# A four-layer graph attention kernel on one core: the last layer's residual on GpSimd, two sets of layer-norm statistics later, attention vectors fetched a group sooner

## Chip, cores and metric

The kernel runs on one core of one Trainium2 chip. The metric is the device time of one execution in microseconds (us), given as the median of several runs. In the profile PE is TensorE (matmuls), PEld its weight loads, DVE is VectorE, ACT is ScalarE, POOL is GpSimd, and SP is the engine whose queue issues nearly all DMAs here. "L389" is line 389 of the kernel before.

## The reference

Sixteen graphs of 1024 nodes with 256 features share one adjacency matrix. Four layers of graph attention follow each other, each with a layer norm ahead of it and a residual after it:

```python
for each layer:
    h = maximum(layernorm(x), 0)
    q = h @ W                                  # layers 0, 2: 4 heads of 64; layers 1, 3: 1 head of 256
    e = leaky_relu(q @ a_src + (q @ a_dst)^T)  # one 1024 x 1024 matrix per head
    attn = softmax(where(adj, e, -inf))
    x = x + act(attn @ q)                      # act: elu in layers 0 to 2, relu in layer 3
```

All is float32. In layer 3 the activation is a plain relu, so its residual is x + max(y, 0).

## The kernel before

**Steps.** A step is one layer of one graph. The 64 steps run in an order written out in `order_of_steps` (L635): four graphs are in flight (streams 0 to 3), and layers of four heads and of one head alternate wherever possible. Counted from n = 0, the first steps are: 0, 1 and 2 are layer 0 of streams 0, 1, 2; 3 is layer 1 of stream 0; 4 is layer 0 of stream 3; 5 and 6 are layer 1 of streams 1 and 2; 7 is layer 2 of stream 0. Steps 0, 1, 2, 4 and 7 have four heads, steps 3, 5 and 6 have one. Steps of layer 3 are n = 10, 12, 14, 16 and so on, 16 in all.

**One step on the engines.** With 1024 nodes on 128 partitions there are C = 8 column blocks.

- *Preparation* (L229). `stats` (L236) runs eight BN_STATS on DVE over x. `combine` and `combine_end` (L259, L277) turn them into a scale and a shift with ten small instructions on POOL. `normalise` (L282) applies both on ACT, one half (four blocks) at a time. From step 2 on the transposing is done by DMA: `split` (L290) separates the 16-bit halves on ACT and issues a DMA transpose on SP, `merge` (L301) puts them together again on ACT. `project` (L321) multiplies with W on PE (L328) and ACT copies each bank out (L330); after each half POOL scales the result (L340). `factors` and `rows` (L344, L349) make the other attention factor, which goes to DRAM and comes back as a broadcast (`fetch`, L367); ACT copies it into PSUM (L384).
- *Weights* (L386). For each head and column block DVE makes one tile of 128 x 1024 attention weights (L389): 32 tiles for a step of four heads, 8 for one of one head. The pool holds 18 such tiles (`WBUFS`).
- *Aggregation* (L393). PE multiplies the tiles with the projected features (L405), in eight groups per step; ACT copies each group's bank out (L420). There are four such PSUM banks (`ps`), shared with the projections.
- *Finish* (L426). In the groups of the following step: DVE takes the reciprocal (L441), POOL divides (L452), and in layers 0 to 2 POOL clips (L454), ACT exponentiates (L458), DVE combines (L464) and POOL adds to x (L465). In layer 3 a single DVE instruction does relu and add (L467). Then `store` (L469) issues the two output DMAs on SP, and behind them the load of the next graph into the same x tile.

**Order.** Every engine works its instructions in program order, and the program writes that order out by hand (`manual_schedule`, L565). The main loop (L611) goes through the groups of all steps; group k of step n has the index 8n + k. In each it emits, in this order: the weight tiles still due, the group's matmuls, the due pieces of the previous step's finish (at L477: group of the following step for divide, two divisions, two exponentials, two adds), then anything in `later`, then the preparation pieces that are due (`prepare`, L496), then weight tiles ahead.

When a preparation piece is due is read from tables (L50 to L57) of 21 numbers, relative to 8(n - 2). Their places are: statistics of half 0, of half 1, the combine of both (used with four heads), normalise half 0, normalise half 1, split 0, merge 0, four projections, split 1, merge 1, four projections, factors, rows, fetch, end. Lines 541 to 557 choose a table for each step. Before the change steps 0 to 2 with four heads use `SOON` (steps 0 and 1 are in fact written out otherwise), later ones `FOUR`, or `SHORT` or `NEXT` when the stream's previous layer ends too late; steps of one head use `ONE` or `TIGHT`. So step 4 uses `FOUR` (base 16: statistics at 8, combine at 11, normalise at 16 and 17) and step 7 uses `SHORT` (base 40: statistics at 36, normalise at 40 and 41).

**Start.** Masks are made from the adjacency matrix in eight blocks (`mask_rows`, L187): fetch, sign on DVE (L197), `turn` by PE into PSUM (L211), `positive` on DVE (L214), `nonzero` on ACT (L218). `order` (L582) interleaves them with the preparation of step 0.

**Vectors of later layers.** `weight_columns` (L134) makes the extra columns of W from the attention vector of a layer in four pieces: `vectors`, a DMA on SP (L143) into a tile of the weight pool; `spread`, a matmul on PE (L150) that copies it to all partitions, and an ACT copy (L153); `columns` on DVE (L160, L161); and `bound` (L169). For layers 1, 2 and 3 they are placed by the loop at L608, at indices 1, 27 and 43 and at 1, 2 and 8 groups after.

Of the kernel before, what the change touches and what calls it, by code (L numbers as in the profile page):

```python
# [32 lines left out]
ALU = mybir.AluOpType  # L33
# [16 lines left out]
FOUR = (-8, -8, -5, 0, 1, 0, 3, 5, 5, 5, 5, 1, 4, 5, 5, 5, 5, 6, 8, 8, 10)  # L50
SHORT = (-4, -4, -4, 0, 1, 0, 3, 5, 5, 5, 5, 1, 4, 5, 5, 5, 5, 6, 8, 8, 10)
NEXT = (-4, -4, -4, 1, 3, 2, 5, 8, 8, 8, 8, 4, 7, 8, 8, 8, 8, 9, 10, 10, 12)
ONE = (2, 2, 2, 3, 4, 3, 5, 7, 7, 7, 7, 4, 7, 8, 8, 8, 8, 8, 11, 11, 12)
SOON = (0, 0, 0, 1, 2, 1, 3, 4, 4, 5, 5, 2, 5, 6, 6, 7, 7, 7, 8, 8, 10)
FIRST = (-4, -4, -4, -2, -0.9, -1, -1, -0.8, -0.8, -0.8, -0.8, 0, 0, 1, 1, 1, 1, 1, 2, 2, 4)
TIGHT = (4, 4, 4, 5, 6, 5, 7, 8, 8, 8, 8, 6, 8, 9, 9, 9, 9, 9, 10, 10, 12)
LATE = (0, 0, 0, 1, 2, 1, 3, 4, 4, 4, 4, 2, 4, 5, 5, 5, 5, 5, 6, 6, 8)  # L57
# [11 lines left out]
def kernel(ctx: ExitStack, tc: tile.TileContext, x, adj, ws, avs, out):  # L69
    nc = tc.nc  # L70
# [38 lines left out]
    L = len(LAYERS)  # L109
# [312 lines left out]
    def slack(n):  # L422

        return LAYERS[steps[n + 1][1]][0] == 1

    def finish(n):  # L426

        b, l = steps[n]
        H = LAYERS[l][0]
        D = F // H  # L430
        st = state[n]

        def views(half):
            s = slice(half * HALF, (half + 1) * HALF)
            return (xs[b][:, s, :].rearrange("p c (h d) -> p (c h) d", h=H),
                    st["y"][:, s, :, 0:D].rearrange("p c h d -> p (c h) d"),
                    st["r"][:, s, :].rearrange("p c h -> p (c h)"))

        def divide():
            st["r"] = small.tile([P, C, H], F32, name="r")  # L440
            nc.vector.reciprocal(st["r"], st["y"][:, :, :, D])  # L441

        def scaled(half):
            xh, yh, r = views(half)
            rb = r[:, :, None].to_broadcast([P, HALF * H, D])
            if l < L - 1:

                e = st["e", half] = prep.tile([P, HALF * H, D], F32, name="rows",
                                                    bufs=HBUFS)
                if H > 1 and slack(n):  # L450
                    nc.vector.scalar_tensor_tensor(e, yh, 0.0, rb, op0=ALU.min, op1=ALU.mult)  # L451
            nc.gpsimd.tensor_tensor(yh, yh, rb, op=ALU.mult)  # L452
            if l < L - 1 and not (H > 1 and slack(n)):
                nc.gpsimd.tensor_scalar(e, yh, 0.0, -3.0e38, op0=ALU.min, op1=ALU.max)  # L454

        def exponential(half):
            if l < L - 1:
                nc.scalar.activation(st["e", half], st["e", half], AF.Exp)  # L458

        def add(half):  # L460
            xh, yh, r = views(half)
            if l < L - 1:
                e = st["e", half]
                nc.vector.scalar_tensor_tensor(e, e, -1.0, yh, op0=ALU.add, op1=ALU.max)  # L464
                nc.gpsimd.tensor_add(xh, xh, e)  # L465
                return
            nc.vector.scalar_tensor_tensor(xh, yh, 0.0, xh, op0=ALU.max, op1=ALU.add)  # L467

        def store(half):  # L469
            nc.sync.dma_start(  # L470
                out=out[b].rearrange("(p c) f -> p c f", p=P)[:, half * HALF:(half + 1) * HALF],
                in_=xs[b][:, half * HALF:(half + 1) * HALF, :])
            if half == 1 and b + STREAMS < B:
                load(b + STREAMS)


        at = (0, 0, 0, 0, 1, 1, 1) if slack(n) and H > 1 else (0, 0, 1, 1, 2, 2, 3)  # L477
        return list(zip(at, (divide, lambda: scaled(0), lambda: scaled(1), lambda: exponential(0),
                             lambda: exponential(1), lambda: add(0), lambda: add(1)))) + (
                    [(4, lambda: store(0)), (4, lambda: store(1))] if l == L - 1 else [])  # L480

# [37 lines left out]
    def emit_heads(i):  # L519

        while done["g"] <= min(i + C // 2, done["tiles"] + C, len(tiles) - 1):
            n, h, _ = tiles[done["g"]]
            if n >= done["prepared"]:
                break
            broadcast(n, h)
            done["g"] += C
            fetch_heads()
# [13 lines left out]
    for n, (b, l) in enumerate(steps):  # L541

        free = -99
        if b % STREAMS in last:
            over = last[b % STREAMS] + 1
            free = 8 * over + (8 if l == 0 else 2 if LAYERS[steps[over][1]][0] == 1 else 4)
        last[b % STREAMS] = n
        start = 8 * (n - 2)
        kind = ONE if LAYERS[l][0] == 1 else SOON if n < 3 else FOUR
        if kind is FOUR and free > start + kind[0]:  # L550
            kind = SHORT if slack(n - 2) else NEXT
        if kind is ONE and free > start + kind[0]:
            kind = TIGHT
        if free > start + kind[0]:
            kind = LATE
            start = max(free, agenda_of[-1][0] + 5, start - LATE[7])
        agenda_of.append([start + k for k in kind] if n > 1 else FIRST)
        if n > 2:


            assert agenda_of[n][7] >= 8 * (n - 2)
            assert agenda_of[n][3] >= agenda_of[n - 1][12]
    ending = []
    later = {}
    with tc.manual_schedule():  # L565
        blocks = [mask_rows(c) for c in range(C)]
        layer = [weight_columns(l) for l in range(L)]
        layer[0][0](nc.scalar)
        load(0, 2)
        load_weights(0)  # L570
        for c in range(C):
            blocks[c][0]()
        load(1)
        load_weights(1)
        for i in range(2, STREAMS):
            load(i)
        nc.scalar.activation(warm, half1, AF.Exp)
        nc.vector.tensor_copy(identb, ident)
        layer[0][1]()
        first = [piece for _, piece in preparation(0)]  # L580

        order = (  # L582

            [first[0], first[1], first[3], lambda: layer[0][2](range(1)), first[2],
             lambda: layer[0][2](range(1, K)), first[5], first[6], first[4], layer[0][3]]

            + [blocks[c][1] for c in range(4)]
            + [first[7], first[8], blocks[0][2], blocks[4][1], blocks[5][1], blocks[0][3],
               first[9], first[10], blocks[1][2], blocks[6][1], blocks[7][1], blocks[1][3],
               first[11], first[12], blocks[2][2], blocks[0][4],  # L590
               lambda: prepare(-4), first[13], first[14], blocks[1][4], blocks[2][3],
               blocks[3][2], first[15], first[16], blocks[3][3]]

            + [first[17], blocks[4][2], first[18], first[19], lambda: emit_heads(0),
               blocks[5][2], blocks[6][2], blocks[4][3], blocks[4][4], blocks[5][3], blocks[5][4],
               blocks[6][3], blocks[7][2], blocks[2][4], blocks[3][4], blocks[7][3],
               lambda: prepare(-2), blocks[6][4], lambda: prepare(-1), blocks[7][4]])
        plan(1)
        planned = 2
        done["prepared"] = 1  # L600
        for piece in order:
            piece()
        emit_tiles(C, must=True)
        prepare(-0.5)
        for i in range(2, STREAMS):
            load_weights(i)

        for l, at in ((1, 1), (2, 8 * 3 + 3), (3, 8 * 5 + 3)):  # L608
            for i, piece in zip((0, 1, 2, 8), layer[l]):
                later[at + i] = piece  # L610
        for n in range(len(steps)):  # L611
            for k, (h, i0, per) in enumerate(groups(n)):
                while planned < len(steps) and min(
                        a[0] for a in agenda_of[planned:planned + 2]) <= 8 * n + k:
                    plan(planned)
                    planned += 1
                emit_tiles(place[n, h, C - 1] + 1, must=True)
                aggregate(n, h, i0, per)
                if i0 + per == C:
                    done["free"] = place[n, h, C - 1] + 1  # L620
                while ending and ending[0][0] <= k:
                    ending.pop(0)[1]()
                upto = min(done["tiles"] + (6 if per > 1 else 3), done["free"] + WBUFS)

                emit_heads(upto - 1 + (C // 2 if per == 1 and k >= C - 2 else 0))
                if 8 * n + k in later:
                    later[8 * n + k]()
                prepare(8 * n + k)
                emit_tiles(upto)
            for _, piece in ending:  # L630
                piece()
            ending = finish(n) if n < len(steps) - 1 else []
# [35 lines left out]
```

## Time and profile before

| what | us |
|---|---|
| median of 3 runs | 2464.47 (2461.95 to 2467.52) |
| the profiled execution's own time | 2463.54 |
| its span, first to last instruction | 2461.8 |
| PE busy on matmuls | 2396.4 (97% of the span) |
| DVE busy | 2041.2 (83%) |
| ACT busy | 1484.9 (60%) |
| POOL busy | 1074.7 (44%) |
| L389, a weight tile on DVE | 1280 of 1.273 each |
| L467, the last layer's residual on DVE | 30 of 1.215 each |
| L452, L454, L465 on POOL | 2.091, 1.041 and 2.365 each |

A group of the profile is one line, engine and shape, with its count, busy time and the mean of one. A "wait" is idle time of an engine just before an instruction, put down to what released it. The chain is followed back from the last instruction to what released each one. A timeline line gives start and duration in us, the engine, the line, what is written and read, the number of instructions, and in brackets the idle time before. Matmul ends are modelled, and a matmul's busy time can contain a slower clock; the granted clock of a stretch is listed with 1.00 for full speed.

### The profile page before, as it was taken

Reading aid. Unit: us, or ns where it says so; the run is one execution under the profiler, and the core shown is the slowest. Engines: PE = TensorE matmul, PEld = TensorE weight load, DVE = VectorE, ACT = ScalarE, POOL = GpSimd, SP = SyncE. Lnnn points to the kernel's source line nnn. Section 1 sums busy time; section 2 is a strip of 40 time slices with the busy share of each in tenths; the row PEclk is TensorE's granted clock in tenths of the full one; section 3 lists DMA queues with packets and bytes.
Section 4 is the critical chain, followed back from the end, with each engine's and each line's share of the span. In section 5 each row is a group of like instructions: output and inputs, shape, how many; then the busy total and the mean of one; then the engine's idle time right before and its main releaser. Section 6 shows DMA issues by size and latency. Waiting matters only on the chain.

```text
span 2461.8 us, 86525 instructions
## 1 busy us (share of the span) xinstructions
PE 2396.4 (97%) x39104; PEld 2150.2 (87%) x39104; DVE 2041.2 (83%) x2138; ACT 1484.9 (60%) x2501; POOL 1074.7 (44%) x1366
## 2 busy tenths in 40 slices
PE   7989999999999999999999999999999999999899
PEld 5888798889898889898898888899988889888878
DVE  8988688888888988888988888988888888888963
ACT  5464676555666656765556765656665556765461
POOL 3344455543345454444343555453444344553341
PEclk9999999999999999999999999999999999999999
DMA  4322232233333322232433332323433422323221
GB/s 181 81 54 62 44 79 62 70 105 90 94 85 87 74 64 56 67 79 88 113 97 81 77 71 62 79 63 80 113 79 87 109 58 54 79 62 70 77 48 61
DMA packets 294761, 193.40 MB, mean 79 GB/s; under 512 B 264182, under 2 KB 266998, under 8 KB 292472
## 3 DMA queue, kind: packets, MB, share of 16 engines
q1 hardware_dynamic: 294382, 187.86, 30.2%
q8 instruction: 306, 5.01, 0.8%
q14 instruction: 63, 0.52, 0.1%
q10 hardware_dynamic: 10, 0.00, 0.0%
HBM read 105.39 MB, written 17.43 MB: 50 GB/s over the span
## 4 chain that ended last, share of the span: by engine, by line
PE 82%; ACT 6%; DVE 5%; DMA 4%; issue 2%; POOL 0%; SPq 0%; DVEq 0%; ACTq 0%
PE bank L405 64%; PE bank L328 18%; DVE w L389 4%; ACT rows L286 2%; DMA gs<-grow 2%; DMA grow<-gT 1%; ACT rows L295 1%; ACT g L384 1%; ACT rows L458 1%; ACT rows L303 1%; DVE bn L241 1%; ACT y L420 0%; DMA rows<-rows 0%; PE bank L352 0%; DVE rows L464 0%
## 5 line engine op out<-in xcount | busy, mean ns | idle before, releaser
L405 PE MATMUL bank<-whx,w 128*64 128x65 f32 x36864 | 1899.5, 240 | 26.4 <-DVE w L389 17.0
L405 PEld LDWEIGHTS bank<-whx,w 128*64 128x64 f32 x36864 | 1746.2, 144 | 186.5 <-issue 22.6
L389 DVE SCALAR_TENSOR_TENSOR w<-g,rcol,mask 128x1024 f32<-128x1024 f32 x1280 | 1538.9, 1273 | 206.1 <-PE bank L405 160.8
L340 POOL TENSOR_TENSOR whx<-whx 128x1024 f32<-128x1024 f32 x128 | 244.9, 1913 | 823.8 <-ACT whx L338 823.8
L420 ACT ACTIVATE y<-bank 128x260 f32<-128x260 f32 (+1 forms) x504 | 191.9, 381 | 567.1 <-PE bank L405 567.0
L328 PE MATMUL bank<-wx,rows 128*128 128x264 f32 (+1 forms) x2048 | 489.3, 393 | 16.0 <-ACT y L420 8.4
L328 PEld LDWEIGHTS bank<-wx,rows 128*128 128x128 f32 x2048 | 384.4, 192 | 92.5 <-ACT y L420 14.2
L452 POOL TENSOR_TENSOR y<-y,r 128x1024 f32<-128x1024 f32 x126 | 262.4, 2091 | 254.0 <-DVE rows L451 186.6
L330 ACT ACTIVATE whx<-bank 128x264 f32<-128x264 f32 (+1 forms) x512 | 193.6, 388 | 194.2 <-PE bank L328 193.5
L286 ACT ACTIVATE rows<-x,shift,rstd 128x256 f32<-128x256 f32 x512 | 264.5, 588 | 72.5 <-POOL shift L280 70.3
L465 POOL TENSOR_TENSOR x<-x,rows 128x1024 f32<-128x1024 f32 x96 | 227.1, 2365 | 181.6 <-DVE rows L464 181.6
L303 ACT ACTIVATE rows<-rows 128x2048 uint16<-128x2048 uint16 x124 | 265.9, 2144 | 21.5 <-DMA rows<-rows 21.5
L295 ACT ACTIVATE rows<-rows 128x2048 uint16<-128x2048 uint16 x124 | 236.9, 1911 | 3.9
L464 DVE SCALAR_TENSOR_TENSOR rows<-rows,y 128x1024 f32<-128x1024 f32 x96 | 187.9, 1957 | 49.1 <-ACT rows L458 43.7
L241 DVE BATCH_NORM_STATS2 bn<-x 128x6 f32<-128x256 f32 x512 | 175.5, 409 | 33.4 <-POOL x L465 30.0
L384 ACT ACTIVATE g<-gs 128x1024 f32<-128x1024 f32 x159 | 162.6, 1023 | 63.8 <-DMA gs<-grow 49.1
L274 POOL TENSOR_TENSOR rstd<-rstd,neghalf 128x4 f32<-128x4 f32 (+1 forms) x97 | 120.3, 1240 | 15.2 <-DVE shift L275 7.8
L458 ACT ACTIVATE rows<-rows 128x1024 f32<-128x1024 f32 x96 | 100.6, 1048 | 2.0 <-POOL rows L454 2.0
L441 DVE RECIPROCAL r<-y 128x32 f32<-128x32 f32 (+1 forms) x63 | 17.2, 274 | 96.3 <-ACT y L420 96.3
L451 DVE SCALAR_TENSOR_TENSOR rows<-y,r 128x1024 f32<-128x1024 f32 x58 | 70.1, 1250 | 1.1
L467 DVE SCALAR_TENSOR_TENSOR x<-y,x 128x1024 f32<-128x1024 f32 x30 | 36.5, 1215 | 8.9 <-POOL y L452 8.9
L338 ACT ACTIVATE whx<-whx,nbias 128x16 f32<-128x16 f32 (+1 forms) x128 | 40.3, 315 | 4.2
(67 smaller groups left out, 444.4 us busy)
## 6 DMA issues: line engine op xcount, KB each, us to landing
gs<-grow SPq DMA_DIRECT2D x159, 512.0 KB
x<-in_x SPq DMA_DIRECT2D x15, 1024.0 KB
out<-x SPq DMA_DIRECT2D x30, 512.0 KB
w<-in_adj SPq DMA_DIRECT2D x8, 512.0 KB
rows<-rows SPq DMA_TRANSPOSE x124
x<-in_x SPq DMA_DIRECT2D x2, 512.0 KB
wx<-in_L_gnn_W SPq DMA_DIRECT2D x8, 128.0 KB
out<-x SPq DMA_DIRECT2D x8, 128.0 KB
```

The lines of the kernel that those rows point to most:

```text
L241: nc.vector.bn_stats(bn[:, c, :], xs[b][:, c, :])
L286: nc.scalar.activation(xn[:, :, q, :], xs[b][:, c, :].rearrange("p (k i) -> p k i", k=K), AF.Relu, bias=st["shift"][:, c:c + 1], scale=st[ ...
L295: nc.scalar.activation(bits, xn.rearrange("p (n s) -> p s n", s=2), AF.Copy)
L303: nc.scalar.activation(st["hT", half].rearrange("p k i -> p (k i)").bitcast(U16).rearrange("p (n s) -> p n s", s=2), st["turned", half].re ...
L328: nc.tensor.matmul(pw, lhsT=st["hT", half][:, k, q * P:(q + 1) * P], rhs=wx[l][:, k, :], start=(k == 0), stop=(k == K - 1))
L330: nc.scalar.activation(st["whx"][:, c, :], pw, AF.Copy)
L340: nc.gpsimd.tensor_tensor(wh[:, :, :, 0:D], wh[:, :, :, 0:D], wh[:, :, :, D:D + 1].to_broadcast([P, HALF, H, D]), op=ALU.mult)
L389: nc.vector.scalar_tensor_tensor(w, state[n]["g", h], state[n]["rcol"][:, jc, h:h + 1], masks[LAYERS[steps[n][1]][3]][:, jc, :], op0=ALU.m ...
L405: nc.tensor.matmul(acc[o % P:o % P + cols, q, :], lhsT=st["w", h, jc][:, o:o + cols], rhs=st["whx"][:, jc, h * (D + 1):(h + 1) * (D + 1)], ...
L420: nc.scalar.activation(st["y"][:, i0:i0 + per, h, :], acc, AF.Copy)
L452: nc.gpsimd.tensor_tensor(yh, yh, rb, op=ALU.mult)
L465: nc.gpsimd.tensor_add(xh, xh, e)
```

## The change

Four edits are made.

1. In layer 3, `scaled` gets one more POOL instruction per half, max(y, 0), and `add` is a POOL add of x and y in place of DVE's combined instruction. The last step, which writes its result in another way (L409), is not concerned.
2. The table `SOON` is changed, and is used for all steps of four heads below n = 8, not below n = 3. So steps 2, 4 and 7 are placed by it. (A guard falls back to `SHORT` where the stream is not free; none of the three needs it.) Step 2 has its merges at 4 and all projections at 5, its factors at 6. Step 4 has its statistics and combine at 16 (was 8 and 11), normalise at 17 and 18 (was 16 and 17), splits at 17 and 18 (16 and 17), merges at 20 and 20 (19 and 20), projections at 21 as before. Step 7 has statistics and combine at 40 (was 36), normalise and splits at 41 and 42 (40 and 41), merges at 44 and 44 (43 and 44), projections at 45 as before.
3. At the start, mask block 5 is turned ahead of step 0's factors and rows, and no longer behind them.
4. The `vectors` piece of layers 2 and 3 is placed at 26 and 42, not 27 and 43; `spread`, `columns` and `bound` keep their places.

```diff
-SOON = (0, 0, 0, 1, 2, 1, 3, 4, 4, 5, 5, 2, 5, 6, 6, 7, 7, 7, 8, 8, 10)
+SOON = (0, 0, 0, 1, 2, 1, 4, 5, 5, 5, 5, 2, 4, 5, 5, 5, 5, 6, 8, 8, 10)
...
             nc.gpsimd.tensor_tensor(yh, yh, rb, op=ALU.mult)
+            if l == L - 1:
+                nc.gpsimd.tensor_scalar(yh, yh, 0.0, 3.0e38, op0=ALU.max, op1=ALU.min)
...
-            nc.vector.scalar_tensor_tensor(xh, yh, 0.0, xh, op0=ALU.max, op1=ALU.add)
+            nc.gpsimd.tensor_add(xh, xh, yh)
...
-        kind = ONE if LAYERS[l][0] == 1 else SOON if n < 3 else FOUR
+        kind = ONE if LAYERS[l][0] == 1 else SOON if n < 8 else FOUR
         if kind is FOUR and free > start + kind[0]:
             kind = SHORT if slack(n - 2) else NEXT
+        if kind is SOON and free > start:
+            kind = SHORT
...
-            + [first[17], blocks[4][2], first[18], first[19], lambda: emit_heads(0),
-               blocks[5][2], blocks[6][2], blocks[4][3], blocks[4][4], blocks[5][3], blocks[5][4],
+            + [first[17], blocks[4][2], blocks[5][2], first[18], first[19], lambda: emit_heads(0),
+               blocks[6][2], blocks[4][3], blocks[4][4], blocks[5][3], blocks[5][4],
...
-        for l, at in ((1, 1), (2, 8 * 3 + 3), (3, 8 * 5 + 3)):
-            for i, piece in zip((0, 1, 2, 8), layer[l]):
+        for l, at in ((1, 1), (2, 8 * 3 + 2), (3, 8 * 5 + 2)):
+            for i, piece in zip((0, 1, 2, 8) if l == 1 else (0, 2, 3, 9), layer[l]):
```

## The prediction, made before the changed kernel ran

> Steps are counted from 0, groups as 8n + k; the "fifth and eighth step" are n = 4 and n = 7. All times are microseconds of the profiled execution before, or are shifted from them.
>
> **What bounds the kernel now.** First the page: busy shares, then the chain that ended last.
>
> ```profile
> PE 2396.4 (97%) x39104; PEld 2150.2 (87%) x39104; DVE 2041.2 (83%) x2138; ACT 1484.9 (60%) x2501; POOL 1074.7 (44%) x1366
> ...
> PE 82%; ACT 6%; DVE 5%; DMA 4%; issue 2%; POOL 0%; SPq 0%; DVEq 0%; ACTq 0%
> ```
>
> PE is the bound; a saving on DVE or ACT counts only where PE waits for it. Second, what PE waited for:
>
> ```profile
> PE bank L405 <- DVE w L389: 17.0, 22, 0.9
> ...
> PE bank L150 <- DMA w<-in_L_gnn_a: 7.0, 3, 4.6
> ```
>
> Third, busy time by stretch. From 299 to 2280 us PE idles 16 of 1981 us, and the waits there name DVE for 0.6 us. So almost nothing can be won in the middle; the edits can count before 299 us and after 2280 us. Fourth, the timelines of those two ends, and the chain around 200 us:
>
> ```profile
> 200.91 2.82 DMA w<-in_L_gnn_a
> 203.73 0.14 issue
> 203.87 1.24 PE bank L150 x2
> ```
>
> PE stands for 1.30 us (202.56 to 203.87) for the attention vector of layer 2. The clock after it:
>
> ```profile
> 202.00:204.00 2.00, 0.70 (x4) 1.00 0.58 210
> 204.00:206.00 2.00, 2.00 (x4) 0.67 0.01 4
> 206.00:208.00 2.00, 2.00 (x6) 0.50 0.16 34
> ```
>
> The column after the busy time is the granted clock: it halves, and the 48 matmuls that follow take 12.11 us where 48 take 10.43 elsewhere, 1.68 us more. DVE at the end:
>
> ```profile
> 2288.04 1.22 DVE L467 SCALAR_TENSOR_TENSOR x<-y,x 128x1024 f32<-128x1024 f32 x1
> 2289.17 2.70 DVE L241 BATCH_NORM_STATS2 bn<-x 128x6 f32<-128x256 f32 x8
> 2291.79 2.46 DVE L389 SCALAR_TENSOR_TENSOR w<-g,rcol,mask 128x1024 f32<-128x1024 f32 x2
> 2294.16 1.21 DVE L467 SCALAR_TENSOR_TENSOR x<-y,x 128x1024 f32<-128x1024 f32 x1
> 2295.30 7.24 DVE L389 SCALAR_TENSOR_TENSOR w<-g,rcol,mask 128x1024 f32<-128x1024 f32 x6
> ```
>
> No gap on DVE, and PE waits tile by tile until 2302.59: both residual adds lie on the path here.
>
> **What the Trainium skill says.** "TensorE: Matmul & The Clock Gate", Part 1: the array runs at half rate after an idle window of about 3.4 us, in windows that run freely. The trace agrees on the half rate and about 3.3 us of it, but 1.30 us of standing was enough at 203.9, while 1.17 us at 287 was not; so a stall may cost 1.7 us more or nothing. "GPSIMD Engine Reference", 4.1: two-input elementwise about twice as slow as VectorE, one-input near line rate. Agrees: L465 2365 ns against L467 1215; L454 1041. Same page, section 1: GpSimd shares its SBUF interface with VectorE instructions of two SBUF inputs. Agrees: L464 takes 1.21 us alone, 2.9 beside L452.
>
> **Part 1, the last layer's residual (15 steps, 30 halves).** DVE loses 30 x 1.215 = 36.5 us. POOL gains per half one TENSOR_SCALAR at 1.04 (L454's row) and one add at 2.37 (L465's row, same shapes): 102 us in all, 6.8 a step. What is queued behind: in a middle step (496 to 519 us) POOL sits idle 20.4 us from the second L452 to the next L340. Added there are one or two scalars and two adds, under 7 us; cover 13 us, and if it were gone each microsecond would cost up to 15 in the kernel. The adds need no lookahead tiles of DVE ahead of them and end near 504, before DVE's 508.4. The two stores (509.08) wait on SP behind the fetch issued at 508.69, so they and the load behind them (516.79) stay. PE gain in the middle: 0. At 2288 the cover is POOL's 7.9 us before the statistics; 1.04 + 2.37 fit. There DVE gets 1.13 + 1.22 = 2.3 us back, PE waits 2.3 less, and the later waits to 2361 hang on the same tiles. **+2.3** (bounds 1 to 2.6: the next g copy on ACT, at 2302.71, moves only about 1.5). In the last step DVE's adds end at 2446.1 and their stores leave by 2449.4; POOL, with two L452, two scalars and two adds (10.6 us) from 2434.8, ends at 2445.4: 0.
>
> **Part 2, block 5 turned earlier.** DVE waits 1.68 us for that block at 33.34, then does three masks. With the block turned behind block 4 (30.4 to 31.0), one mask of 1.15 us runs inside the wait; the next waits for block 6 (33.2) as before. DVE starts its tiles 1.15 us sooner and has no gap from 36.94 to 159 us, so this carries on. Step 2's new places (all projections at 5, merges at 4) fall where PE waits for DVE: 0, unless the merge at 4 keeps ACT from the g copy that DVE needs at 81 (I find 0.5 us to spare; loss up to 1).
>
> **Part 3, step 4's statistics from group 8 to 16.** The 8 BN_STATS (2.65 us at 100.36) leave the stretch in which PE waits for DVE (109 to 137 us). With part 2, step 2's first group ends at 137.4, not 141.2. ACT's normalise and split of step 4 (148.0 to 151.9) no longer stand before the evictions of step 3's projections, so group 2 of step 2 starts at 148.7, not 154.44: 5.7 us won so far. Then it is given back. POOL does, in program order, L452, L454, L340 (to 147.5) and only then step 4's combine (4.2 us, as at 49.41 to 53.60): 151.7. ACT: normalise and split to 155.75, evict and exponential, second normalise and split to 161.25. On SP the two transposes now stand around step 3's store and fetch of its g row (issued near 160, 165.74 before), which step 3 needs only at 170: no cost. A transpose lands 5.2 to 6.2 us after its split (876.7 to 882.2, 2066.65 to 2072.85): 166.75. Merge 2.15, g copy 1.0, then the eviction of group 5: 170.2. PE ends group 5 at 164.6, has banks for three projections (0.92 each, to 167.4), stands 2.8 us, needs five more: 174.8, or 176.5 with a half clock. Before: 177.26. **+1.5** (0 to 5.3, the upper end without the stall).
>
> **Part 4, vectors a group sooner, layer 2.** At group 26 they stand behind the g fetch that goes out near 198, not the one at 200.46; 2.82 us of transfer end near 201.3, before PE is done at 202.56. Both the 1.30 and the 1.68 go. Late next: merge of step 5 at 213.3, projections would start at 214.3. **+3.0** (0 to 3.0). Layer 3: at group 42 the fetch is behind the first transpose of step 7, which now leaves at 283 (part 5) and takes 1.9 to issue; it lands at 286.7, against 286.96. +0.4 at most.
>
> **Part 5, step 7's statistics from 36 to 40.** In the trace they run on DVE at 253.03, after the last tile of step 4: no wait of PE ends there, so nothing is won. Moved, the combine stands on POOL behind two L452 and step 6's second L340, which waits for ACT until 273.0: 279.1 instead of 260. ACT's normalise starts there, not at 273.44; second split to 287.4, landing 292.9, merge 295.05, g copy, eviction of group 5 at 296.35. PE has issued three projections by 294.0, stands 2.35 and ends at 300.95, or 302.6 at half clock, against 298.98. **-3.0** (+0.4 to -4).
>
> **Sum.** 2.3 + 1.5 + 3.0 - 3.0 = 3.8 us. The profiled execution took 2463.54 (span 2461.8, 1.7 around it): 2459.7. It lies 0.9 below the median of the runs (2464.47), so I forecast **2460.6**, 0.16% less. A measurement tells about 0.2% (4.9 us, 2459.5) from no change.
>
> **Rivals.** (B) The stalls of parts 3 and 5 do not form: transposes or combine come earlier than worked out. For it: steady steps split and merge two groups apart with PE waiting 0 to 1 us; against: POOL's order is fixed by the program. 5.3 + 3.0 + 0.4 + 2.3 = 11.0: 2453.5; with one stall of two some 2457.5. (C) Slower: the second halves of steps 4 and 7 land later still. Place: SP's in-order queue, where one transpose took 5.31 us to issue at 71.02 instead of 1.9 and the g fetches stand between. Each microsecond of delay costs two, one per step; with 3.8 to use up, slower by 4.9 needs 4.4 us at each, a landing 9.9 us after the split. 2470. Against it: no landing over 6.2 us is seen where a merge waited. (D) The vector fetch does what it says but lands no sooner (it still queues behind a fetch): 2.3 + 1.5 - 3.0 = 0.8: 2463.7.
>
> **Chances.** Forecast (2458 to 2464) 0.50, of it 0.15 under 2459.5; B 0.30, nearly all faster; C 0.10, 0.08 of it slower; D 0.10, same. Faster 0.43, same 0.49, slower 0.08. Range 2453 to 2465: it takes in B's end and D, leaves C.
>
> **What would show it.** Right: no PE wait at L150 near 200 us and full clock there; L389 without L467 between at about 2288 and PE there 2.3 us earlier; PE waits on L328 of 2 to 3 us in steps 2 and 5, released by ACT, with half clocks after. No wait at L328 in those two steps, with ACT's normalise starting the moment it is issued and not when POOL releases it, speaks for B. Wrong altogether: PE waits in steps 11 to 17 that name POOL, or stores that leave later than the g fetch before them.

## The result and the profile after

The changed kernel takes **2471.36 us** in the median of 16 runs, the kernel before 2465.21 beside it (16 runs): ratio **1.0021**, 95% interval 1.0013 to 1.0030. It is slower by about 5 us. The forecast was 2460.6 us, 0.16% less than before. The profiled execution after took 2468.03 us (span 2466.1), 4.5 us more than the one before.

The page, in the two lines that were read before: DVE has lost its 30 residual instructions and POOL has gained 170 us, but PE is as busy as it was, and still holds the chain of work that ended last (81%, 82% before).

```profile
PE 2398.5 (97%) x39104; PEld 2152.4 (87%) x39104; DVE 2010.0 (82%) x2108; ACT 1485.7 (60%) x2501; POOL 1245.1 (50%) x1426
...
PE 81%; DVE 6%; ACT 5%; DMA 5%; issue 2%; POOL 1%; SPq 0%; DVEq 0%; ACTq 0%; POOLq 0%
```

What PE waited for in the changed kernel (total, times, longest):

```profile
PE bank L328 <- ACT y L420: 17.0, 12, 4.4
PE bank L405 <- DVE w L389: 12.9, 18, 0.9
...
PE bank L150 <- DMA w<-in_L_gnn_a: 4.9, 1, 4.9
...
PE bank L150 <- ACT y L420: 1.8, 1, 1.8
```

The waits for DVE (17.0 before) and for the vectors (7.0, 3 times, before) are smaller, as intended. The first line is new in size: before it had 8.4 us, the longest 2.5. L328 is the projection; it waits because its PSUM bank is not yet copied out, and the copy, L420, is on ACT.

**Where the time went.** PE transposes one row tile per step (L352); the start of that instruction in both traces dates each step. After minus before, in us (minus is sooner):

| from the transpose of step ... to that of ... | change in this stretch | forecast |
|---|---|---|
| start to 1 (mask block) | -2.3 | -1.15 |
| 1 to 2 (second projections of step 2) | +2.8 | 0 |
| 2 to 4 (statistics and merges of step 4) | +0.9 | -1.5 from the start to step 4, mask included |
| 4 to 5 (vectors of layer 2) | -3.0 | -3.0 |
| 5 to 6 | +1.4 | 0 |
| 6 to 7 (step 7) | +4.3 | +3.0, less 0.4 |
| 7 to 60 (middle) | +2.2 | 0 |
| 60 to 63 (end) | -2.0 | -2.3 |

The sum is +4.3; the spans differ by 4.4. The end and the vectors came out as forecast. The losses stand in steps 2, 4 and 7, whose places are changed. Two rows hold chance of one execution, too. In the first, three of the five traces without the mask edit (res_only, vec_only, step7_vec) are ahead of the kernel before, too, by 1.1 to 1.5 us. And the +1.4 from step 5 to 6 goes with a half clock from 250.5 us that lasts 6.83 us, where the kernel before has one of 3.41.

**The stall in step 2's group 5** (changed kernel; timeline, the lines of ACT and PE that concern it: start, duration, engine, line; in brackets the idle time before and what ended it):

```profile
169.10 2.14 ACT L303 ACTIVATE rows<-rows 128x2048 uint16<-128x2048 uint16 x1 [3.89 <-DMA rows<-rows]
171.15 1.00 ACT L384 ACTIVATE g<-gs 128x1024 f32<-128x1024 f32 x1
172.10 0.36 ACT L420 ACTIVATE y<-bank 128x260 f32<-128x260 f32 x1
...
172.51 6.15 PE L328 MATMUL bank<-wx,rows 128*128 128x264 f32 x20 [3.85 <-ACT y L420]
```

L303 is the second merge of step 4. ACT reaches it at 165.2 and stands 3.89 us for its DMA transpose. The g copy (L384) and the eviction (L420) are behind it in ACT's program, although what the eviction copies was ready long before: PE ended its three projections at 168.66 and stands 3.85 us for that bank. Then the 20 matmuls of the five projections left take 6.15 us, where 20 take 4.72 at full clock later in the trace. The kernel before does all eight projections (32 matmuls) at this place without a stop:

```profile
169.88 7.39 PE L328 MATMUL bank<-wx,rows 128*128 128x264 f32 x32
```

The same picture stands earlier in the changed kernel, in step 0's groups, with step 2's second merge, which begins at 76.92:

```profile
76.92 2.15 ACT L303 ACTIVATE rows<-rows 128x2048 uint16<-128x2048 uint16 x1 [5.07 <-DMA rows<-rows]
78.98 1.00 ACT L384 ACTIVATE g<-gs 128x1024 f32<-128x1024 f32 x1
79.92 0.36 ACT L420 ACTIVATE y<-bank 128x260 f32<-128x260 f32 x1
80.01 7.25 DVE L389 SCALAR_TENSOR_TENSOR w<-g,rcol,mask 128x1024 f32<-128x1024 f32 x6 [1.05 <-ACT g L384]
...
80.34 6.15 PE L328 MATMUL bank<-wx,rows 128*128 128x264 f32 x20 [4.37 <-ACT y L420]
```

Here DVE, too, waits for the g copy, 1.05 us. The split ahead of that transpose ended at 68.0, and the merge could start at 76.9, 9 us later: on SP its issue stood behind two g fetches until 68.93 and took 4.54 us.

**Step 7** loses in another way, ahead of its projections:

```profile
279.00 2.07 ACT L286 ACTIVATE rows<-x,shift,rstd 128x256 f32<-128x256 f32 x4 [2.41 <-POOL shift L280]
...
287.15 0.37 ACT L420 ACTIVATE y<-bank 128x257 f32<-128x257 f32 x1
287.54 1.52 PE L150 MATMUL bank<-w,ones 1*128 1x512 f32 x2 [1.78 <-ACT y L420]
...
288.98 6.64 PE L405 MATMUL bank<-whx,w 128*128 128x257 f32 x16
```

POOL releases the normalise at 279.00, as worked out (279.1). ACT then normalises and splits twice without a pause to 287.15, an eviction is due inside that, and PE's matmul at L150, which needs the bank, stands 1.78 us. The kernel before stood there for the vectors' DMA:

```profile
287.10 1.09 PE L150 MATMUL bank<-w,ones 1*128 1x512 f32 x2 [1.17 <-DMA w<-in_L_gnn_a]
288.12 3.74 PE L405 MATMUL bank<-whx,w 128*128 128x257 f32 x16
```

What follows costs more than the stall. The clock, of the changed kernel (stretch, length, PE busy and matmuls, granted clock, DMA share, GB/s):

```profile
204.00:206.00 2.00, 2.00 (x7) 1.00 0.30 102
...
288.00:290.00 2.00, 2.00 (x4) 0.52 0.81 156
...
294.00:296.00 2.00, 2.00 (x9) 0.78 0.24 90
```

Around 204 us the clock is full now, and the stall for the vectors of layer 2 is gone: that is the 3.0 us of part 4. From 288 it is halved, and the 16 matmuls take 6.64 us instead of 3.74.

Both costs can be summed over two-microsecond stretches from 40 to 312 us: PE's idle time, and PE's busy time times one minus the granted clock. Before: 17.3 idle and 8.1 lost to the clock. After: 19.9 and 12.0. So of the 6.5 us that this stretch got worse, 3.9 are clock.

**DVE at the end** of the changed kernel, where two L467 stood among the tiles:

```profile
2289.59 4.85 DVE L389 SCALAR_TENSOR_TENSOR w<-g,rcol,mask 128x1024 f32<-128x1024 f32 x4
2294.36 2.70 DVE L241 BATCH_NORM_STATS2 bn<-x 128x6 f32<-128x256 f32 x8
2296.97 9.62 DVE L389 SCALAR_TENSOR_TENSOR w<-g,rcol,mask 128x1024 f32<-128x1024 f32 x8
```

The tiles follow each other, and the next transposes are 2.0 us nearer than before.

### The profile page after: what moved, and what is told of

It is laid out like the page before. It is cut to its first block, busy times and chain, and to the rows that moved or that the text cites. A ratio compares the mean times of both kernels' runs of the same rounds, so it can differ in the third digit from the quotient of the medians.

```text
span 2466.1 us, 86566 instructions
## 1 busy us (share of the span) xinstructions
PE 2398.5 (97%) x39104; PEld 2152.4 (87%) x39104; DVE 2010.0 (82%) x2108; ACT 1485.7 (60%) x2501; POOL 1245.1 (50%) x1426
## 4 chain that ended last, share of the span: by engine, by line
PE 81%; DVE 6%; ACT 5%; DMA 5%; issue 2%; POOL 1%; SPq 0%; DVEq 0%; ACTq 0%; POOLq 0%
PE bank L405 63%; PE bank L328 17%; DVE w L389 4%; DMA gs<-grow 2%; DMA grow<-gT 2%; ACT rows L286 2%; ACT rows L295 1%; DMA rows<-rows 1%; ACT g L384 1%; ACT rows L460 1%; DVE bn L241 1%; ACT rows L303 0%; ACT y L420 0%; PE bank L352 0%; DVE w L160 0%
## 5 line engine op out<-in xcount | busy, mean ns | idle before, releaser
L405 PE MATMUL bank<-whx,w 128*64 128x65 f32 x36864 | 1901.5, 241 | 24.9 <-DVE w L389 12.9
L405 PEld LDWEIGHTS bank<-whx,w 128*64 128x64 f32 x36864 | 1747.8, 144 | 184.5 <-issue 26.5
L420 ACT ACTIVATE y<-bank 128x260 f32<-128x260 f32 (+1 forms) x504 | 191.6, 380 | 564.7 <-PE bank L405 564.7
L328 PE MATMUL bank<-wx,rows 128*128 128x264 f32 (+1 forms) x2048 | 489.1, 393 | 22.7 <-ACT y L420 17.0
L328 PEld LDWEIGHTS bank<-wx,rows 128*128 128x128 f32 x2048 | 385.2, 192 | 99.2 <-ACT y L420 22.9
L467 POOL TENSOR_TENSOR x<-x,rows 128x1024 f32<-128x1024 f32 x96 | 227.1, 2366 | 174.6 <-DVE rows L466 174.6
L303 ACT ACTIVATE rows<-rows 128x2048 uint16<-128x2048 uint16 x124 | 265.9, 2145 | 30.1 <-DMA rows<-rows 28.2
L384 ACT ACTIVATE g<-gs 128x1024 f32<-128x1024 f32 x159 | 162.6, 1023 | 65.1 <-DMA gs<-grow 56.1
L454 POOL TENSOR_SCALAR y<-y 128x1024 f32<-128x1024 f32 x30 | 109.0, 3633 | 2.6
L469 POOL TENSOR_TENSOR x<-x,y 128x1024 f32<-128x1024 f32 x30 | 65.4, 2202 | 0.0
```

What stands on the lines that cost most here:

```text
L303: nc.scalar.activation(st["hT", half].rearrange("p k i -> p (k i)").bitcast(U16).rearrange("p (n s) -> p n s", s=2), st["turned", half].re ...
L328: nc.tensor.matmul(pw, lhsT=st["hT", half][:, k, q * P:(q + 1) * P], rhs=wx[l][:, k, :], start=(k == 0), stop=(k == K - 1))
L405: nc.tensor.matmul(acc[o % P:o % P + cols, q, :], lhsT=st["w", h, jc][:, o:o + cols], rhs=st["whx"][:, jc, h * (D + 1):(h + 1) * (D + 1)], ...
L420: nc.scalar.activation(st["y"][:, i0:i0 + per, h, :], acc, AF.Copy)
```

## The experiments

Theory after the result: the new places put a second merge on ACT ahead of an eviction; ACT holds its whole queue for the transpose, PE stands for the bank, and the clock halves after. Rivals: the residual on POOL slows the middle (+2.2 us stand there); a stall in one step only replaces one in a later step; the losses are chance of the clock. Every kernel computes the whole reference. Each ratio is against the kernel before on the same chip, whose medians were 2462.0, 2459.4, 2460.6 and 2460.9 us in the four sets. In kernels with a table of their own (STEP) all lines after it are one higher: L328 is L329, L420 is L421.

**1. Residual, mask and vectors, all places old** (old_tables).

```diff
-SOON = (0, 0, 0, 1, 2, 1, 4, 5, 5, 5, 5, 2, 4, 5, 5, 5, 5, 6, 8, 8, 10)
+SOON = (0, 0, 0, 1, 2, 1, 3, 4, 4, 5, 5, 2, 5, 6, 6, 7, 7, 7, 8, 8, 10)
...
-        kind = ONE if LAYERS[l][0] == 1 else SOON if n < 8 else FOUR
+        kind = ONE if LAYERS[l][0] == 1 else SOON if n < 3 else FOUR
```

> Everything of the change except the tables: steps 2, 4 and 7 are placed as before. Theory (the new places make ACT hold a merge for a transpose while PE's bank waits for an eviction behind it, in steps 0, 2 and 5): with those stalls gone the residual's 2.3 us, the vector's 3.0 and some of the mask's 1.15 to 2.3 remain: 5 to 7 us faster than before, so 0.9972 to 0.998. Rival (the residual on GpSimd costs time in the middle steps, where the trace after loses another 2.2 us between 340 and 2290): about 1.0 to 1.001.

Measured: 2459.07, ratio 0.9994 [0.9985, 1.0003]. At step 7's transpose it is 4.3 us ahead of the kernel before, of it 3.0 at the vectors, and the interval of its ratio lies below that of the change (1.0013 to 1.0030). So the loss is in the table. But the time lies between what theory and rival expected: the lead is gone by step 50, and only the end's 2.0 are left.

**2. The residual alone** (res_only): the `scaled` and `add` lines of the diff in the kernel before.

> Only the last layer's residual moved to GpSimd. Theory (tables): the prediction's 2.3 us at the end come out, 0.9991, no loss in the middle. Rival (residual): slower, 1.001 or more, with PE later by 2 us between 340 and 2290.

Measured: 2461.08, ratio 0.9994 [0.9985, 1.0004]. From the transpose of step 7 to that of step 60 it drifts by +1.9 us, but mask_only, which has no residual on POOL, drifts by +2.3 there. Of all the traces the eight with the residual on POOL change by -3.0 to +4.6 us in this stretch against the kernel before (mean +0.5), the five without it by -3.6 to +3.8 (mean +0.2). From 60 to 61 it wins 2.1. The rival asked for 1.001 or more, and the interval ends below that: no harm of POOL in the middle shows, and that rival falls.

**3. The new table for steps below 3 alone** (step2_only).

```diff
-SOON = (0, 0, 0, 1, 2, 1, 3, 4, 4, 5, 5, 2, 5, 6, 6, 7, 7, 7, 8, 8, 10)
+SOON = (0, 0, 0, 1, 2, 1, 4, 5, 5, 5, 5, 2, 4, 5, 5, 5, 5, 6, 8, 8, 10)
```

> Only step 2's places are changed (merges at 4, all projections at 5). Theory (tables): PE stands some 4 us at step 2's fourth projection, released by ACT's eviction, and VectorE loses about 2 us waiting for the g copy behind that merge; about 2.5 us slower, 1.001. Rival (residual): VectorE was the bound there, PE's stall is hidden: 1.000.

Measured: 2465.51, ratio 1.0013 [1.0004, 1.0022]. From the transpose of step 1 to that of step 2 it loses 4.6 us, with PE idle 5.0 us at L328 for L420. The "0" of the prediction is wrong.

**4. The new table for steps 4 and 7 alone** (steps47_only), the vectors still at 27 and 43.

```diff
+STEP = (0, 0, 0, 1, 2, 1, 4, 5, 5, 5, 5, 2, 4, 5, 5, 5, 5, 6, 8, 8, 10)
...
-        kind = ONE if LAYERS[l][0] == 1 else SOON if n < 3 else FOUR
+        kind = ONE if LAYERS[l][0] == 1 else SOON if n < 3 else STEP if n < 8 else FOUR
```

> Only steps 4 and 7 are placed by the new table; step 2 keeps its places. Theory (tables): wins 2.6 us by step 4's statistics, loses about 3.5 at the end of step 2 and 4 to 5 in step 5: 4 to 6 us slower, 1.0016 to 1.0025. Rival (residual): at most 1 us, 1.0004.

Measured: 2473.84, ratio 1.0049 [1.0034, 1.0064], worse than expected. One line of its timeline says why:

```profile
293.13 2.04 PE L151 MATMUL bank<-w,ones 1*128 1x512 f32 x2 [6.02 <-DMA w<-in_L_gnn_a]
```

At 43 the vectors' DMA is on SP behind the second transpose of step 7, which now leaves later; the two transposes took 6.22 us to issue from 284.40, and PE stands 6.02 us for the vectors. So the move of layer 3's vectors to 42, which the prediction priced at 0.4 us or less, is what step 7's new places cannot do without.

**5. The change, with the second merge a group later** (merge_later), in steps 2, 4 and 7.

```diff
-SOON = (0, 0, 0, 1, 2, 1, 4, 5, 5, 5, 5, 2, 4, 5, 5, 5, 5, 6, 8, 8, 10)
+SOON = (0, 0, 0, 1, 2, 1, 4, 5, 5, 5, 5, 2, 5, 6, 6, 6, 6, 7, 8, 8, 10)
```

> The changed kernel, with the second merge of steps 2, 4 and 7 one group later, behind the first four projections, and the last four projections and the factors a group later. Theory (ACT holds the second merge for its transpose, and the eviction that PE's fourth projection needs stands behind it): the stalls of 4.4 us in step 0 and 3.9 us in step 2 go, of step 5 most; with the gains that stay, 0.998 to 0.9995 of before. Rival (steps 2, 4 and 7 simply start too late, or the bound has gone to the combine on GpSimd): PE waits as long, now for the merge itself, and the time stays at 1.0015 to 1.0025.

Measured: 2456.71, ratio 0.9991 [0.9983, 0.9999]. The waits at L328 in the groups of steps 0 and 2 are gone, and from the transpose of step 2 to that of step 4 it wins 4.6 us. Two others are left: 3.62 us at L405 in step 0, and 3.96 us at L150 in step 5 with a half clock after it (from 6 to 7: +6.1); most of step 5's stall was expected to go. The interval lies wholly below that of the change. So the merge, with the projections, factors and rows that go with it, was a cause, but not of the loss of step 7.

**6. Step 4 alone late, with the later merge** (step4_late): experiment 1, and step 4 by the table of experiment 5.

```diff
+STEP = (0, 0, 0, 1, 2, 1, 4, 5, 5, 5, 5, 2, 5, 6, 6, 6, 6, 7, 8, 8, 10)
...
+        kind = ONE if LAYERS[l][0] == 1 else SOON if n < 3 else STEP if n == 4 else FOUR
```

> Residual, vectors and mask as in the change; step 2 and step 7 placed as before; step 4 with the late statistics, its second merge one group later. Theory: the statistics' 2.6 us are kept and not given back: 1.5 to 3 us faster than the same without step 4's move (0.9994 in the first call), 0.9982 to 0.999 of before. Rival: step 4's normalise, waiting for the combine, still costs what the statistics win: 0.9994 or more.

Measured: **2449.35** (5 runs), ratio **0.9964** [0.9952, 0.9977]. It beats both kernels, and by more than expected. ACT and PE in step 2's groups 5 and 6:

```profile
163.34 3.83 PE L329 MATMUL bank<-wx,rows 128*128 128x264 f32 x16
164.90 0.37 ACT L421 ACTIVATE y<-bank 128x260 f32<-128x260 f32 x1
...
168.21 2.14 ACT L304 ACTIVATE rows<-rows 128x2048 uint16<-128x2048 uint16 x1
170.98 3.83 PE L329 MATMUL bank<-wx,rows 128*128 128x264 f32 x16
```

The eviction at 164.90 stands ahead of the merge, which starts at 168.21 without waiting for its transpose; neither projection waits or runs at half clock. From 40 to 312 us PE idles 13.4 us and loses 4.7 to the clock, 7.3 less than before.

**7. Step 4 late with the change's own table** (step4_tight): experiment 6 with the second merge, its projections, factors and rows one group sooner, and nothing else.

```diff
-STEP = (0, 0, 0, 1, 2, 1, 4, 5, 5, 5, 5, 2, 5, 6, 6, 6, 6, 7, 8, 8, 10)
+STEP = (0, 0, 0, 1, 2, 1, 4, 5, 5, 5, 5, 2, 4, 5, 5, 5, 5, 6, 8, 8, 10)
```

> Kernel: the residual on POOL, the vectors a group sooner, the mask block sooner, steps 2 and 7 at their old places, and step 4 at the places that the change gives it. It differs from step4_late in one table row: the second merge, the last projections, the factors and the rows of step 4 stand one group sooner. Theory (the tight second merge holds ACT ahead of an eviction): a wait of PE at L329 of 3 to 5 us in step 2, released by ACT's L421, and step 3's row transpose to step 4's some 4 to 6 us later than in step4_late (from -6.6 to about -1 against the kernel before); ratio 0.998 to 0.9992. Rival (step4_late is fast for another reason, such as the places of steps 2 and 7 being old, or the phase of the clock): no such wait, and a ratio within 0.0008 of step4_late's 0.9964.

Measured: 2460.83, ratio 1.0000 [0.9992, 1.0008], 0.36% above experiment 6. Its timeline has the wait back:

```profile
167.47 2.14 ACT L304 ACTIVATE rows<-rows 128x2048 uint16<-128x2048 uint16 x1 [4.15 <-DMA rows<-rows]
...
170.46 0.37 ACT L421 ACTIVATE y<-bank 128x260 f32<-128x260 f32 x1
...
170.88 7.61 PE L329 MATMUL bank<-wx,rows 128*128 128x264 f32 x20 [4.45 <-ACT y L421]
```

One row of the table moves the transpose of step 4 from 6.2 us ahead of the kernel before to 1.2 behind it: 4.45 us of waiting, and 2.9 of half clock (7.61 less 4.72). That is 7.4 us, where 4 to 6 were expected, and the ratio, too, is above the expected 0.998 to 0.9992. The later merge, with what follows it, is what makes experiment 6 fast; that rival falls. So does chance of the clock as the cause: it moves single executions, but the intervals of these two kernels, of several runs each, lie clear of each other.

**8. The change, step 2 put back** (step2_old): old SOON for steps below 3, the change's table for steps 4 and 7 (STEP of experiment 7, `n < 8`).

> Kernel: the change, with step 2 alone put back to its old places (steps 4 and 7 at the new ones). Theory: the wait of 4.4 us at L328 in step 0, with the half clock behind it, goes, and step 2's row transpose stands 1.5 to 2.5 us sooner than before's, not 0.5 later; steps 4 and 7 lose what they lose in the change. So 2 to 4 us less than the change: ratio 1.0002 to 1.0015. Rival (step 2's new places only move a wait that the following steps would have had anyway): the gain is gone by step 4's row transpose, ratio 1.002 as in the change.

Measured: 2465.21, ratio 1.0014 [1.0006, 1.0021]. The wait of 4.4 us in step 0 goes, and at the transpose of step 2 this kernel is 2.2 us ahead of the change. At that of step 4 it is 0.4 ahead: PE gets to its three projections sooner, but the transpose of step 4 doesn't, so the stall grows from 3.85 to 4.83 us and its half clock is 1.1 us longer (7.25 against 6.15). The intervals of the two ratios overlap. Most of what step 2 costs is thus no separate loss: the next stall takes it in. Half of the theory's step fails here, and the rival of this run has the better of it.

**9. The vectors alone** (vec_only), and **10. vectors and step 7** (step7_vec).

```diff
-        for l, at in ((1, 1), (2, 8 * 3 + 3), (3, 8 * 5 + 3)):
-            for i, piece in zip((0, 1, 2, 8), layer[l]):
+        for l, at in ((1, 1), (2, 8 * 3 + 2), (3, 8 * 5 + 2)):
+            for i, piece in zip((0, 1, 2, 8) if l == 1 else (0, 2, 3, 9), layer[l]):
```

> Only the vectors of layers 2 and 3 a group sooner. Theory: PE's wait for layer 2's vector goes, with or without the half clock behind it, and 1.2 us of layer 3's: 2 to 4.2 us, 0.9983 to 0.9992. Rival (the fetch stands on SP behind another): 1.0000.

> Step 7 placed by the new table and the vectors a group sooner, nothing else. Theory: 3.0 us won in step 3 and 4 lost in step 5: 1.0000 to 1.0008, with PE level or 1 to 2 us late from step 7 on. Rival (step 7's late statistics cost nothing, the loss in step 5 comes from the earlier stalls): 0.9985 to 0.999.

Measured: vec_only 2460.21, ratio 1.0008 [1.0000, 1.0016]; a miss. The wait near 200 us is gone and 3.0 us are won from step 4 to 5, but 2.8 of them are lost by step 7: the half clock from about 248 lasts 6.83 us, where that of the kernel before (from about 252) lasts 3.41, and there is another from about 285, where PE stood 1.16 us at L150 (1.17 before, at full clock). That wait was expected to go, too; but the DMA of layer 3's vectors, though placed a group sooner, still leaves SP behind both transposes of step 7, which take SP from 274.68 to 282.60. Experiment 10 has this edit and the change's table for step 7 (STEP, `n == 7`). It gives 2462.62, ratio 1.0013 [1.0005, 1.0020], slightly over the expected 1.0000 to 1.0008: the wait at L150 is 3.42 us, released by L420, and there is almost none at the fourth projection (0.45).

**11. The mask block alone** (mask_only).

> Kernel: only block 5 of the mask turned ahead of step 0's factors and rows. The prediction's step (1.15 us sooner on DVE, carried on to 159 us): step 2's row transpose 1.0 to 1.5 us sooner, ratio 0.9995 or so, hardly to be told from 1. Rival: DVE starts its tiles no sooner, since the row copies of step 0 on PE and ACT now stand behind the block: landmark within 0.4 us, or later by up to 1.

Measured: 2461.72, ratio 1.0005 [0.9997, 1.0014]. DVE's masks of this kernel:

```profile
32.41 2.35 DVE L214 TENSOR_SCALAR mask<-bank 128x1024 uint8<-128x1024 bf16 x2 [0.56 <-PE bank L211]
34.88 7.24 DVE L389 SCALAR_TENSOR_TENSOR w<-g,rcol,mask 128x1024 f32<-128x1024 f32 x6
```

The wait of 1.68 us has become 0.56, 1.1 us as predicted; the tiles start 2.06 us sooner, 0.9 of it because the first blocks arrive sooner in this execution. The lead holds to step 31, then drifts to +0.1 by step 55, and the time isn't better.

**12. The clip to a tile of its own** (relu_apart): experiment 6, and `max(y, 0)` written to a `rows` tile.

```diff
-                nc.gpsimd.tensor_scalar(yh, yh, 0.0, 3.0e38, op0=ALU.max, op1=ALU.min)
+                nc.gpsimd.tensor_scalar(e, yh, 0.0, 3.0e38, op0=ALU.max, op1=ALU.min)
...
-            nc.gpsimd.tensor_add(xh, xh, yh)
+            nc.gpsimd.tensor_add(xh, xh, st["e", half])
```

> Kernel: step4_late, with the last layer's max(y, 0) on POOL written to a tile of its own (name rows) and added from there, instead of in place in y. In the changed kernel that TENSOR_SCALAR (y<-y, L454) took 3.63 us, where the prediction counted 1.04 from the clip of the other layers (rows<-y). If writing in place is what costs 2.6 us, it takes 1.04 here; if it is the order of max and min or their constants, 3.6 again. Time: POOL's residual is on no path in the middle, so within 0.001 of step4_late's 0.9964 against the kernel before; if instead the slow scalar costs something anywhere, 0.995 or less. The tiles named rows are shared with the splits and merges, so a new wait of ACT for POOL would show as later merges and a slower kernel.

Measured: 2450.22, ratio 0.9955 [0.9943, 0.9968] (6 runs), like experiment 6, so its gain stands in a second set of runs. The clip on POOL in this kernel (line, operation, count, busy, mean ns, idle before):

```profile
L454 POOL TENSOR_SCALAR rows<-y 128x1024 f32<-128x1024 f32 x30 | 109.0, 3632 | 2.6
```

Still 3.63 us: writing in place isn't the reason.

## Why the prediction was wrong

**Sum.** The chain of ratios old_tables, step4_tight, step2_old, change adds one part each: 0.9994, 1.0000, 1.0014, 1.0021 (on three chips, each against the kernel before there). In us (0.1% is 2.46): residual, mask and vectors together -1.5; step 4 +1.5; step 7 +3.4; step 2 +1.7. Each term is uncertain by 2 to 3 us, as the intervals say. The forecast had, with the mask's gain counted in step 4: -5.3, -1.5, +3.0, 0. So it is short by 3.8 in the gains, 3.0 in step 4, 1.7 in step 2 and 0.4 in step 7. For steps 4 and 2 the traces show what failed. The gains are open: the trace of experiment 1 has 4.3 us of them at step 7's transpose and 2.0 at the end, but its median has 1.5 (at most 3.7 by the interval). That trace loses 4.6 us between steps 7 and 60, as much as executions scatter there (below); whether the gains are lost regularly, and where, no run shows.

**Part 3, the step that failed**: PE "stands 2.8 us, needs five more: 174.8, or 176.5 with a half clock. Before: 177.26", from which "+1.5". The mechanism was right, its size was not. Experiment 7 shows it undisturbed by step 2: ACT's normalise at 151.42 (151.7 worked out), second split done at 160.73 (161.25), merge at 167.47 (166.75), bank free at 170.8 (170.2). Those four are within 0.7 us. But PE was ready at 166.4, not at 167.4, so it stood 4.45 us, and the half clock after cost 2.9, not nothing to 1.7; the five projections ended at 178.5. The +1.5 lies between the prediction's two ends, 2.5 us ahead of 177.26 without a half clock and 0.8 with one; they ended 1.2 behind it. Of the 3.7 us between 174.8 and 178.5, 2.9 are the half clock, 0.7 the bank's later release, 0.1 the projections. The mis-sized term is thus the price of the half clock. What PE gains ahead of such a stall does not end it sooner, since its end is set by POOL's combine, two splits and a landing; the gain lengthens the stall, and with it the stretch of idle PE that halves the clock.

**Part 2, "Step 2's new places (all projections at 5, merges at 4) fall where PE waits for DVE: 0"**: failed. The sentence named the danger, the merge at 4 that holds the g copy, but put its loss at 1 at most, and asked only for DVE. DVE did wait 1.05 us for it. But in ACT's queue behind the g copy stands also the eviction that PE's fourth projection needs, and the transpose took 9 us from split to landing. PE lost 2.8 us there (4.6 in experiment 3), though experiment 8 shows that most of it would have been lost in step 4. The mask's 1.15 was right (1.1).

**Part 5, "-3.0"**: nearly right in size (-4.3 in the trace), wrong in its place. The normalise started to 0.1 us where it was put, but the transposes landed within 4.5 us of the second split and no projection waited. The loss is 0.6 us more at L150, where the two normalises and splits hold the eviction, and 3.3 of half clock after it (16 matmuls 2.9, L150 itself 0.4).

**Part 4, "+3.0"**: right in the trace (2.98), though its 1.68 us of half clock are 1.59 if both groups of 48 matmuls are taken from start to start of what follows (12.02 and 10.43). Alone it did not shorten the median: experiment 9.

**Part 1, "+2.3"**: right at the end (1.8 to 2.1 from step 60 to 61), and 0 in the middle. Its price was not: POOL's scalar took 3.63 us where 1.04 was taken from L454's row, the add 2.20 where 2.37 was. POOL gained 30 x 5.83 = 175 us, not 102. The cover that was named held it, at 2288 with 0.90 us of the 7.9 left; in the last step but one POOL's adds end at 2454.9, 5 us later than worked out and shifted, still 11 us ahead of the end.

**The middle and the clock.** From 312 to 2284 us PE idles 16.0 us in the kernel before, 19.0 in the changed one, 19.8 in mask_only and 14.8 in vec_only. The last two have the program of the kernel before there, so a spread of 5 us is chance of one execution, and the +2.2 of the middle can't be told from it. For the same reason a gain of 3 us by one profile says little of the median.

**Rivals.** B (2453.5, no stalls) did not come. C named nearly the time (2470), but it asked for second halves that land 4.4 us later still in both steps; in step 7 they landed sooner, in step 4 6.5 us after the split, where 5.2 to 6.2 was taken. What it described, a slow issue on SP behind g fetches, did come, but in step 2, which it left out (9 us). The loss was neither the landing nor SP alone, but what ACT holds up while it waits. D did not come.

**The half clock.** "TensorE: Matmul & The Clock Gate", Part 1, of the Trainium skill gives the half rate after an idle window of about 3.4 us, in windows that run freely, and was cited. Taking its cost as "1.7 us more or nothing" from one case was too little, as the clock records of the traces show. In each of the 14 traces all changes of the clock stand on one grid of 3.413 us: the half clocks of the kernel before begin at 204.68 and 252.47 (14 periods apart), those of the changed one at 172.02 and 250.53 (23 periods apart). A half clock lasts one or two periods (once three): the five from 80 to 300 us in the changed kernel last 3.41, 3.41, 3.41, 6.83 and 6.83 us. And a period of the grid need not be all idle. From 45 us to 3.5 us before the end, 65 of the 69 falls to half clock follow a period in which PE was busy for at most 0.52 of the time, and of 9720 periods after which the clock stayed full none was below 0.50; of the other four falls (0.59 to 0.66) three hold the matmul at L150, which reads a single row. The clock comes back after a half-clock period in which PE was busy for 0.80 or more; of 22 after which it stayed half, 19 had 0.79 or less, and the other three hold L150. That is why the stall of step 4 cost 1.4 us of half clock in the changed kernel and 2.9 in experiment 7. PE by periods of the grid (stretch, length, busy and matmuls, granted clock, DMA share, GB/s), first the changed kernel, then experiment 7:

```profile
168.61:172.02 3.41, 0.05 (x1) 1.00 0.01 2
172.02:175.43 3.41, 2.92 (x7) 0.50 0.00 0
...
166.53:169.94 3.41, 0.00 (x0) 1.00 0.08 16
169.94:173.35 3.41, 2.47 (x6) 0.50 0.00 0
173.35:176.76 3.41, 3.41 (x10) 0.50 0.00 0
```

After its stall the changed kernel is busy for 0.86 of the first half-clock period, and the clock comes back; experiment 7 is busy for 0.72 of it, and a second one follows. An estimate from these figures: a full stop of 3.4 us or more empties half of some period wherever it falls, and so always costs a half clock; a shorter one costs it or not by its place in the grid, which differs from execution to execution.

**Open.** Where the gains of parts 1, 2 and 4 went in the medians. Why the clip with max first takes 3.6 us and the one with min first 1.04: in place is excluded, the order of the operations and the constants were not tried apart. Whether vec_only is slower than the kernel before or equal: its interval begins at 1.

## What to carry to other kernels

When work is moved later on one queue, look at what is *behind* it there: a merge that waits for a DMA holds every PSUM copy that follows it, and PE then stands for a bank that has long been full. Put the instruction that waits for a transfer behind the copies that PE needs next; one group later was worth 0.36% here (step4_tight against step4_late). When a stall ends at a fixed time, what is won ahead of it is won for nothing, and the slow clock after it is part of its price: 1.4 to 2.9 us here for stalls of 3.9 to 5.0 us, by where they fell in the grid of 3.41 us.

## What the runs showed that was not expected

- A POOL TENSOR_SCALAR with two operations on 128 x 1024 float32 takes 1.04 us as min with 0, then max, and 3.63 as max with 0, then min, in place or not. The Trainium skill, "GPSIMD Engine Reference", 4.1, has one-input work near line rate; the first agrees, the second is 3.5 times that.
- Whether a stall of about 1.2 us halves the clock is not set by its length: 1.17 us at L150 did not in the kernel before, 1.16 at the same instruction did in vec_only (3.74 against 5.29 us for the 16 matmuls that follow). It is set by its place in the grid of 3.41 us. The first lies across an edge, at 286.60, and the matmuls of L405 fill 0.80 and 0.56 of the two periods; the second lies inside one period, of which they fill 0.40.
- A DMA transpose from SBUF to SBUF took at most 4.5 us (step 7), 6.5 and 6.7 (step 4) and 9 us (step 2) from the end of its split, with its issue on SP taking from 1.9 us (step 7) to 4.5 (step 2); the 5.2 to 6.2 of steady steps is no bound.
